# A four-layer image network on one Trainium2 core: in the last layer's recurrence, both channel halves share one tile of two PSUM banks, and the turn, copy and store of the results move one step on

## The chip, the cores and the metric

The program runs on one core of one Trainium2 chip. The metric is the device time of one execution in microseconds (us); lower is better. Shown are the median of three runs and one further execution that the hardware profiler recorded.

Engines: PE (TensorE, with its weight loads listed apart as PEld), DVE (VectorE), ACT (ScalarE), POOL (GpSimd) and SP (SyncE, which here only issues DMAs). Each takes its instructions in program order. [...]

## The reference

Four layers run one after the other on an image of shape 2 x 128 x 128 x 128 (fp32), each as `x + layer(group_norm(x))`. The change touches only the last one, a two-dimensional selective scan. Its centre, for each of 4 directions, 256 channels d and 16 states n:

```python
delta = softplus(dts + bias)
def step(h, (ut, dt, bt, ct)):
    h = exp(dt * A) * h + (dt * ut) * bt
    y = einsum('bkdn,bkn->bkd', h, ct)
```

The four directions are two orders of the pixels (rows first, columns first), each forward and backward. The four results are brought back to pixel order and added.

## The kernel before

`program` (L1768) calls the layers in turn. The recurrence is `layer3_scan` (L1228 to L1650). It works through 256 **parts** of 512 pixels: 2 images, 2 orders, forward and then backward, 16 strips, 2 halves of a strip. So the parts come in eight runs of 32: forward (`k` 0 or 1) and backward (`k` 2 or 3) by turns. This document calls the forward parts *plain* and the backward ones *turned*, because only the backward ones are turned to pixel order at their end: a plain part's result goes to scratch `yc` in DRAM as it is, and a backward part reads it again (`yf`), adds it, turns the sum with PE transposes (`unturn`), copies it out of PSUM on ACT and stores it to `ys` (`store`).

A part is 8 **slots**. A slot scans 4 tiles of 128 rows (32 channels x 4 states) x 512 pixels. Slot number `s` within a part is 2*q + e: q picks four of the 16 states, e the half of the 256 channels. One turn of the loop over `g` (L1632) issues, in this order:

1. the steps placed at "head";
2. `exponentials(g+1)`: four ACT Exp operations (L1544), tile `da`, from `db`;
3. `kept(g-1)`: an ACT copy of the last column of the finished scans to `states` (L1620), which waits for DVE's scans of slot g-1;
4. the steps at "mid";
5. `products(g+2)`: `but` = delta*u times b, mostly on ACT (L1568, six or seven a slot), the rest on POOL (L1563, one or two a slot). Slots 2q and 2q+1 both read the tiles made for both, so slot 2q needs what is issued only one turn earlier;
6. `weighted(g-1)`: POOL multiplies `hs` by c (L1626);
7. `tiles(g)`: for each j of 4, PE turns four pieces of `but` into one PSUM bank `ups` (L1600, three banks), DVE scans it (L1608), then the steps placed at j follow;
8. `sums(g-2)`: PE adds up the states into `yps` (L1582);
9. the steps at "end".

`in_order` (L114) fixes this order on every engine. The other work is a table of steps `(r, place, step)`: step of part i is issued in turn g = 8i + r. Since a part is 8 turns, r modulo 8 tells the slot of the scan beside which it runs; "slot 5" below means that slot of whichever part is being scanned. In order:

- `load_x` (-15), `load_u` (-10): DMAs in. `project(0)`, `project(1)` (-10, places 1 and 2): PE matmuls to `xdps` (L1332); `projected` (-9, head): ACT copy to `xd` (L1341) and the DMA of `cd`.
- `turn_b`, `ranks(0)`, `ranks(1)` (-8): PE to `btps` (L1350) and `dtps` (L1364). `softplus_a` (-7, head): on ACT two Abs (L1375), one Exp (L1376). `turned_b` (L1357), `softplus_b` (L1382): DVE. `softplus_c` (-6, mid): ACT Ln (L1388).
- `softplus_d(0)`, `(1)` (L1396), `softplus_e(0)`, `(1)` (L1403) in slot 2 and `softplus_f(0)`, `(1)` (L1412) in slot 3: DVE, one operation for each channel half, in place on `dtps` and then on `dl`. `spread` (-5, place 2): DMAs `dl` to DRAM `dd` and back, spread over the partitions, to `db` (L1424); likewise `cd` to `cb`.
- `turn(0)`, `turn(1)` (-4): PE transposes of `dl` to `dltps` (L1439). `turned(0)`, `turned(1)` (-3, slot 5): DVE, `du` = u times `dltps` (L1449).
- `load_forth` (6, end): `yf`. `skip(0)`, `skip(1)` (9 and 10, place 3): DVE, to `ysb` (L1471 plain, L1476 turned).
- `unturn(0)`, `unturn(1)` (13, places 2 and 3: slot 5): for plain parts the `yc` DMA, for turned parts eight PE transposes to `ytps` (L1500). `store` (14, head: slot 6), turned parts only: two ACT copies to `yt` (L1510) and the `ys` DMA (L1513).

PSUM: `ups` has 3 banks, `yps` 2, and pool `ps_m` 3 banks under one tag "misc", taken in turn by `xdps`, `btps`, the two `dtps`, the two `dltps` and the two `ytps`. A tile that comes fourth waits until the readers of the first are done.

Of the kernel before, what the change touches and what calls it, by code (L numbers as in the profile page):

```python
# [9 lines left out]
F32 = mybir.dt.float32  # L10
AF = mybir.ActivationFunctionType
ALU = mybir.AluOpType
PSUM = bass.MemoryType.PSUM
DRAM = bass.MemoryType.DRAM

P = 128
# [96 lines left out]
@contextmanager  # L113
def in_order(tc):  # L114

    cur = tc.nc.cur_bb
    first = len(cur.bb.instructions)
    mark = cur.bb.instructions[first - 1]
    yield
    assert tc.nc.cur_bb is cur  # L120
    traced = list(cur.bb.instructions)
    start = next(k for k in reversed(range(len(traced))) if traced[k] is mark) + 1
    last = {}
    for i in traced[start:]:
        prev = last.get(i.engine)
        if prev is not None:
            tc.add_manual_dep(
                i, prev.name,
                mybir.DependencyInfo(mybir.DependencyClass.NoSync, mybir.DependencyReason.DATA),
                reason="in_order",  # L130
            )
        last[i.engine] = i
# [1095 lines left out]
def layer3_scan(tc, cs, ins, xs, xst, yc, ys):  # L1228
# [11 lines left out]
    nc = tc.nc  # L1240
    NS, DR, NX, T = 16, 8, 40, 512
    with ExitStack() as ctx:
        pool = lambda name, bufs, **kw: ctx.enter_context(tc.tile_pool(name=name, bufs=bufs, **kw))
        w = pool("l3b_w", 1)
        one = pool("l3b_one", 1)
        two = pool("l3b_two", 2)
# [2 lines left out]
        five = pool("l3b_five", 5)  # L1249
        ps_u = pool("l3b_ps_u", 3, space=PSUM)  # L1250
        ps_y = pool("l3b_ps_y", 1, space=PSUM)
        ps_m = pool("l3b_ps_m", 3, space=PSUM)
        dr = pool("l3b_dr", 3, space=DRAM)
        tc.keep_in_program_order(
            nc.scalar.preload_act_table_set("natural_log_exp_and_others")
# [7 lines left out]
        dtw = w.tile([65, 4, 256], F32, name="dtw")  # L1263
        nc.sync.dma_start(dtw, ins["dt_ext"])
        xds = []
        for i in range(2):
            t = w.tile([65, T], F32, name=f"xd{i}")
# [25 lines left out]
        held = {}  # L1293

        def tag_of(i):
            return "_".join(map(str, parts[i]))
# [57 lines left out]
        def turned_b(i):  # L1354
            v = held[i]
            v["bt"] = two.tile([P, 4, NX], F32, name=f"bt_{tag_of(i)}", tag="bt")
            nc.vector.tensor_copy(v["bt"], v["bps"])  # L1357

        def ranks(e):
            def f(i):  # L1360
                k = parts[i][1]
                v = held[i]
                ps = ps_m.tile([P, T], F32, name=f"dtps_{tag_of(i)}_{e}", tag="misc")
                nc.tensor.matmul(  # L1364
                    ps, dtw[:, k, e * P : (e + 1) * P], v["xd"], start=True, stop=True
                )
                v.setdefault("dps", []).append(ps)
            return f


        def softplus_a(i):
            v = held[i]
            ae = one.tile([P, 2, T], F32, name=f"ae_{tag_of(i)}", tag="ae")
            for e in range(2):
                nc.scalar.activation(ae[:, e, :], v["dps"][e], AF.Abs)  # L1375
            nc.scalar.activation(ae, ae, AF.Exp, scale=-1.0)  # L1376
            v["ae"] = ae

# [9 lines left out]
            nc.scalar.activation(dl, v["up"], AF.Ln)  # L1388
            v["dl"] = dl

        def softplus_d(e):

            def f(i):
                v = held[i]
                ps = v["dps"][e]
                nc.vector.scalar_tensor_tensor(ps, ps, 0.0, v["ae"][:, e, :], ALU.max, ALU.add)  # L1396
            return f

        def softplus_e(e):
            def f(i):  # L1400
                v = held[i]
                ps = v["dps"][e]
                nc.vector.scalar_tensor_tensor(  # L1403
                    ps, v["up"][:, e, :], -1.0, ps, ALU.add, ALU.subtract
                )
            return f

        def softplus_f(e):
            def f(i):
                v = held[i]  # L1410
                dl = v["dl"][:, e, :]
                nc.vector.tensor_tensor(dl, dl, v["dps"][e], ALU.subtract)  # L1412
            return f

        def spread(i):

# [15 lines left out]
        def turn(g):  # L1432
            def f(i):
                v = held[i]
                tps = ps_m.tile([P, 2, 2, P], F32, name=f"dltps_{tag_of(i)}_{g}", tag="misc")
                for j in range(2):
                    for e in range(2):
                        p0 = (2 * g + j) * P
                        nc.tensor.transpose(tps[:, j, e, :], v["dl"][:, e, p0 : p0 + P], cs.ident)  # L1439
                v.setdefault("tps", []).append(tps)  # L1440
            return f

        def turned(g):

            def f(i):
                v = held[i]
                if g == 0:
                    v["du"] = two.tile([P, 4, 256], F32, name=f"du_{tag_of(i)}", tag="du")
                nc.vector.tensor_tensor(  # L1449
                    v["du"][:, 2 * g : 2 * g + 2, :], v["ut"][:, 2 * g : 2 * g + 2, :],  # L1450
                    v["tps"][g].rearrange("p j e d -> p j (e d)"), ALU.mult,
                )
            return f

        def load_forth(i):

# [6 lines left out]
        def skip(e):  # L1463
            def f(i):
                k = parts[i][1]
                v = held[i]
                if e == 0:
                    v["ysb"] = one.tile([P, 2, T], F32, name=f"ysb_{tag_of(i)}", tag="ysb")
                ysb, yps = v["ysb"], v["yps"]
                if k < 2:  # L1470
                    nc.vector.scalar_tensor_tensor(  # L1471
                        ysb[:, e, :], v["xc"][:, e, :], dsk[:, 0, k, e : e + 1], yps[e],
                        ALU.mult, ALU.add,
                    )
                else:
                    nc.vector.tensor_tensor(ysb[:, e, :], v["yf"][:, e, :], yps[e], ALU.add)  # L1476
            return f

        def pixels_of(i):


            b, k, s, sub = parts[i]
            i0 = 8 * s + 4 * sub
            if k % 2 == 0:
                return ys[b, 0].rearrange("(i j) d -> j i d", j=P)[:, i0 : i0 + 4, :]
            return ys[b, 1].rearrange("(j i) d -> j i d", i=P)[:, i0 : i0 + 4, :]

        def unturn(g):
            def f(i):
                b, k, s, sub = parts[i]  # L1490
                if k < 2:
                    if g == 0:
                        nc.sync.dma_start(yc[b, k, s, sub], held.pop(i)["ysb"])
                    return
                v = held[i]
                tps = ps_m.tile([P, 2, 2, P], F32, name=f"ytps_{tag_of(i)}_{g}", tag="misc")
                for j in range(2):
                    for e in range(2):
                        p0 = (2 * g + j) * P
                        nc.tensor.transpose(tps[:, j, e, :], v["ysb"][:, e, p0 : p0 + P], cs.ident)  # L1500
                v.setdefault("ytps", []).append(tps)
            return f

        def store(i):
            if parts[i][1] < 2:
                return
            v = held.pop(i)
            yt = one.tile([P, 4, 256], F32, name=f"yt_{tag_of(i)}", tag="yt")
            for g in range(2):
                nc.scalar.copy(  # L1510
                    yt[:, 2 * g : 2 * g + 2, :], v["ytps"][g].rearrange("p j e d -> p j (e d)")
                )
            nc.sync.dma_start(pixels_of(i), yt)  # L1513


# [3 lines left out]
            (-10, 1, project(0)), (-10, 2, project(1)), (-9, "head", projected),  # L1519
            (-8, 0, turn_b), (-8, 1, ranks(0)), (-8, 2, ranks(1)),  # L1520
            (-7, "head", softplus_a), (-7, 0, turned_b), (-7, 2, softplus_b),
            (-6, "mid", softplus_c), (-6, 0, softplus_d(0)), (-6, 1, softplus_d(1)),
            (-6, 2, softplus_e(0)), (-6, 3, softplus_e(1)),
            (-5, 0, softplus_f(0)), (-5, 1, softplus_f(1)), (-5, 2, spread),
            (-4, 0, turn(0)), (-4, 1, turn(1)), (-3, 0, turned(0)), (-3, 1, turned(1)),
            (6, "end", load_forth), (9, 3, skip(0)), (10, 3, skip(1)),
            (13, 2, unturn(0)), (13, 3, unturn(1)),
            (14, "head", store),
        ]

        def at(g, place):
# [97 lines left out]

        slots = 8 * len(parts)  # L1630
        with in_order(tc):
            for g in range(-15, slots + 7):  # L1632
                at(g, "head")
                if 0 <= g + 1 < slots:
                    exponentials(g + 1)
                if 0 <= g - 1 < slots:
                    kept(g - 1)
                at(g, "mid")
                if 0 <= g + 2 < slots:
                    products(g + 2)  # L1640
                if 0 <= g - 1 < slots:
                    weighted(g - 1)
                if 0 <= g < slots:
                    tiles(g)
                else:
                    for j in range(4):
                        at(g, j)
                if 0 <= g - 2 < slots:
                    sums(g - 2)
                at(g, "end")  # L1650
# [230 lines left out]
```

## Time and profile before

| | us |
|---|---|
| median of 3 runs (18427.80 to 18434.36) | 18432.44 |
| profiled execution | 18430.42 |
| its span, first to last instruction | 18428.6 |
| mean granted TensorE clock | 0.918 |

Busy time over the whole span: PE 14403.4 (78%), PEld 8312.0 (45%), DVE 15967.4 (87%), ACT 14862.3 (81%), POOL 11820.0 (64%).

The recurrence lies between about 6200 and 17920 us of the span; the 40 slices of the page show DVE, ACT and POOL at 9 tenths through all of it. Within one run of 32 parts the profile is periodic, with about 45 us a part, and the eight runs differ only by their kind.

How to read the lines further down. A group's line gives the code line, engine, operation, output <- input, shapes and count; after the first bar busy time and the mean ns of one; after the second the engine's idle time just before them and what ended it. A timeline's line gives the start (us), how long it took, the engine, the code line and operation, how many alike follow one another, and in brackets the idle time before and what ended it. Operations on one engine overlap a little at their ends, so the distance from start to start is shorter than the recorded length. A window's line gives, for a stretch of time, each engine's busy time and instruction count, the clock that was granted to TensorE (1.00 is full) and the DMA load.

### The profile page before, as it was taken

What the parts mean: (1) busy time and instruction counts of PE and PEld (TensorE: products, weight loads), DVE (VectorE), ACT (ScalarE), POOL (GpSimd) and SP (SyncE); (2) the same over time, 40 slices, a digit from 0 to 9 for tenths busy, and PEclk for the clock granted to TensorE, in tenths of its full rate; (3) what the DMA queues carried; (4) which work ended last, traced back from release to release, by engine and by line L of the source; (5) the groups of instructions that cost most, each with busy time, mean ns of one, the idle gap of its engine ahead of it and who ended that gap; (6) DMA issues with size and microseconds to landing.
All of it is one profiled execution on the core that took longest, in us unless ns stands there. A gap on an engine that the chain in (4) does not pass through costs nothing. (4 is left out here: it accounts for less than half of the span.)

```text
span 18428.6 us, 277686 instructions
## 1 busy us (share of the span) xinstructions
PE 14403.4 (78%) x97794; PEld 8312.0 (45%) x97794; DVE 15967.4 (87%) x20729; ACT 14862.3 (81%) x30049; POOL 11820.0 (64%) x6490
## 2 busy tenths in 40 slices
PE   7888888887568777777777777777777777777778
PEld 5555555664223344444444444444444444344445
DVE  5776666336889899999999999999999999999996
ACT  4665666334455799999999999999999999999984
POOL 0000000011000499999999999999999999999981
PEclk9999999889779889999999999999999999999989
DMA  2000000111114544444444455544444444445546
GB/s 44 24 23 23 16 18 15 61 64 56 56 48 163 164 116 117 123 126 129 126 115 115 115 126 128 129 123 120 115 122 127 127 124 119 121 118 129 127 129 192
DMA packets 1232639, 1859.34 MB, mean 101 GB/s; under 512 B 124877, under 2 KB 591565, under 8 KB 1228942
## 3 DMA queue, kind: packets, MB, share of 16 engines
q1 hardware_dynamic: 1157374, 1817.40, 37.3%
q10 hardware_dynamic: 73872, 24.16, 0.5%
q8 instruction: 777, 12.73, 0.3%
q14 instruction: 616, 5.05, 0.1%
HBM read 1396.64 MB, written 444.60 MB: 100 GB/s over the span
## 5 line engine op out<-in xcount | busy, mean ns | idle before, releaser
L1608 DVE TENSOR_TENSOR_SCAN hs<-da,states,ups 128x512 f32<-128x512 f32 x8192 | 9926.5, 1266 | 259.9 <-PE ups L1600 248.6
L1626 POOL TENSOR_TENSOR hs<-hs,cb 128x2048 f32<-128x2048 f32 x2048 | 9407.3, 4593 | 314.1 <-POOL but L1563 184.1
L1600 PE MATMUL ups<-ident,but 128*128 128x128 f32 x32768 | 5573.6, 301 | 2587.5 <-DVE hs L1608 1726.5
L1600 PEld LDWEIGHTS ups<-ident,but 128*128 128x128 f32 x32768 | 3865.2, 150 | 6191.5 <-DVE hs L1608 3549.3
L1568 ACT ACTIVATE but<-du,bt 128x256 f32<-128x256 f32 x12800 | 5329.2, 498 | 5.1 <-DVE du L1449 4.2
L1544 ACT ACTIVATE da<-db,na 128x512 f32<-128x512 f32 x8192 | 5224.8, 710 | 24.1 <-DMA db<-dd 20.0
L1582 PE MATMUL yps<-hs,sel 128*32 128x512 f32 x16384 | 2484.5, 682 | 61.4 <-POOL hs L1626 47.6
L1563 POOL TENSOR_TENSOR but<-du,bt 128x256 f32<-128x256 f32 x3584 | 2150.1, 621 | 17.7 <-DVE du L1449 17.7
L306 POOL TENSOR_TENSOR xres<-xres,rowb 128x256 f32<-128x256 f32 x128 | 94.5, 739 | 2445.8 <-DMA xres<-in_x 1810.3
L391 ACT COPY pT<-tps 128x512 f32<-128x512 f32 x1280 | 722.1, 584 | 1115.8 <-PE tps L386 1115.8
L386 PE MATMUL tps<-ident,s 128*128 128x128 f32 x8192 | 1228.9, 287 | 433.5 <-DVE pT L389 269.3
L358 DVE CUSTOM_DVE_ANT_1 s<-sps,relbias 128x512 f32<-128x512 f32 x2048 | 1321.6, 683 | 138.9 <-PE sps L341 133.6
L386 PEld LDWEIGHTS tps<-ident,s 128*128 128x128 f32 x8192 | 900.2, 144 | 1028.7 <-issue 499.6
L371 ACT ACTIVATE s<-s,nm 128x1024 f32<-128x1024 f32 x1024 | 1163.7, 1138 | 129.7 <-DVE nm L369 126.6
L1139 POOL MEMSET xpad<- 128x34 f32 x8 | 1.3, 162 | 1242.7 <-PE xs L1030 1178.8
L341 PE MATMUL sps<-kc,qT 32*128 32x512 f32 x4096 | 619.8, 673 | 1.9 <-DVE qT L326 1.2
L1620 ACT COPY states<-hs 128x4 f32<-128x4 f32 x2048 | 381.5, 186 | 273.3 <-DVE hs L1608 273.3
L389 DVE COPY pT<-tps 128x512 f32<-128x512 f32 x768 | 528.2, 688 | 57.3 <-PE tps L386 54.9
L1582 PEld LDWEIGHTS yps<-hs,sel 128*32 128x32 f32 x16384 | 339.5, 114 | 485.7 <-issue 303.4
L1332 PE MATMUL xdps<-xc,xpw 128*40 128x512 f32 x1024 | 540.5, 610 | 12.4 <-POOL xd L1269 12.4
L1364 PE MATMUL dtps<-xd,dtw 65*128 65x512 f32 x1024 | 539.8, 609 | 0.0
L734 POOL TENSOR_TENSOR xr<-xr,row_ln_b 128x512 f32<-128x512 f32 x64 | 81.1, 1269 | 705.4 <-DMA xr<-x 312.5
(287 smaller groups left out, 16213.1 us busy)
## 6 DMA issues: line engine op xcount, KB each, us to landing
db<-dd SPq DMA_DIRECT2D x1024, 512.0 KB
cb<-cd SPq DMA_DIRECT2D x1024, 256.0 KB
xc<-xs SPq DMA_DIRECT2D x256, 512.0 KB
dd<-dl SPq DMA_DIRECT2D x256, 512.0 KB
ut<-xst SPq DMA_DIRECT2D x128, 512.0 KB
yc<-ysb SPq DMA_DIRECT2D x128, 512.0 KB
yf<-yc SPq DMA_DIRECT2D x128, 512.0 KB
ys<-yt SPq DMA_DIRECT2D x128, 512.0 KB
```

The lines of the kernel that those rows point to most:

```text
L341: nc.tensor.matmul(sps, v["qT"][hp, qt * P : (qt + 1) * P], kc[b, wh + g][hp, ww : ww + 2].rearrange("p a r c -> p (a r c)"), start=True, ...
L358: nc.vector.tensor_tensor_reduce(blocks(v["s", qt][:, h, 512 * g : 512 * g + 512]), blocks(v["sps", qt, g][h]), bias[:, h, :, r0 : r0 + WS ...
L371: nc.scalar.activation(s[:, h, :], s[:, h, :], AF.Exp, bias=nm[:, 2, h : h + 1], scale=-1.0, accum_out=v["sums"][:, qt, h : h + 1],)
L386: nc.tensor.transpose(tps[:, j, :], v["s", qt][:, h, k0 : k0 + P], cs.ident)
L391: nc.scalar.copy(dst, tps)
L1544: nc.scalar.activation(da[:, j, :], held[i]["db"][:, 4 * e + j, :], AF.Exp, scale=na[:, k, c : c + 1])
L1563: nc.gpsimd.tensor_tensor(but[:, j, :, n, :], du[:, tb], bt[:, tb, c : c + 1].unsqueeze(2).to_broadcast([P, 8, 32]), ALU.mult,)
L1568: nc.scalar.activation(but[:, j, :, n, :], du[:, tb], AF.Copy, scale=bt[:, tb, c : c + 1])
L1582: nc.tensor.matmul(v["yps"][e][32 * j : 32 * j + 32, :], sel, hs[:, j, :], start=(q == 0), stop=(q == 3),)
L1600: nc.tensor.transpose(ups[:, tb * P : (tb + 1) * P], v[("but", q, tb // 2)][:, tb % 2, 4 * e + j].rearrange("p n c -> p (n c)"), cs.ident,)
L1608: nc.vector.tensor_tensor_scan(o, a, u, state[:, c0 + j : c0 + j + 1], ALU.mult, ALU.add)
L1626: nc.gpsimd.tensor_tensor(hs, hs, v["cb"][:, s // 2, :].unsqueeze(1).to_broadcast([P, 4, T]), ALU.mult)
```

## The change

`ps_m` keeps one bank "misc" for `xdps` and `btps`; its other two banks become one tile "pair" (`two_banks`), held by `dtps`, then `dltps`, then `ytps`. Each of these now has both halves in one tile, and every pair of operations that read them becomes one operation over 1024 columns: one Abs on ACT, one each of softplus_d, e and f and of `turned` on DVE, one `yt` copy on ACT. The matmuls and transposes stay what they were in number and size.

Steps that merge take the first one's place: d at (-6, 0), e at (-6, 2), f at (-5, 0), turned at (-3, 0). `unturn(0)`, `unturn(1)` go from (13, 2) and (13, 3) to (14, 0) and (14, 1), that is from slot 5 to slot 6, where `project(0)` (place 1, listed earlier, so ahead of `unturn(1)`) and `project(1)` (place 2) run too. `store` goes from the head of slot 6 to the head of slot 7, behind `projected`. The loop runs one turn longer.

```diff
-        ps_m = pool("l3b_ps_m", 3, space=PSUM)
+        ps_m = pool("l3b_ps_m", 1, space=PSUM)
...
+        def two_banks(i, name):
+            return ps_m.tile([P, 2, T], F32, name=f"{name}_{tag_of(i)}", tag="pair")
...
-                ps = ps_m.tile([P, T], F32, name=f"dtps_{tag_of(i)}_{e}", tag="misc")
+                if e == 0:
+                    v["dps"] = two_banks(i, "dtps")
                 nc.tensor.matmul(
-                    ps, dtw[:, k, e * P : (e + 1) * P], v["xd"], start=True, stop=True
-                )
-                v.setdefault("dps", []).append(ps)
+                    v["dps"][:, e], dtw[:, k, e * P : (e + 1) * P], v["xd"], start=True, stop=True
+                )
...
-            for e in range(2):
-                nc.scalar.activation(ae[:, e, :], v["dps"][e], AF.Abs)
+            nc.scalar.activation(ae, v["dps"], AF.Abs)
...
+            nc.vector.scalar_tensor_tensor(ps, ps, 0.0, v["ae"], ALU.max, ALU.add)
...
+            nc.vector.scalar_tensor_tensor(ps, v["up"], -1.0, ps, ALU.add, ALU.subtract)
...
+            nc.vector.tensor_tensor(v["dl"], v["dl"], v["dps"], ALU.subtract)
...
+            nc.vector.tensor_tensor(flat(v["du"]), flat(v["ut"]), flat(v["tps"]), ALU.mult)
...
-            for g in range(2):
-                nc.scalar.copy(
-                    yt[:, 2 * g : 2 * g + 2, :], v["ytps"][g].rearrange("p j e d -> p j (e d)")
-                )
+            nc.scalar.copy(flat(yt), flat(v["ytps"]))
             nc.sync.dma_start(pixels_of(i), yt)
...
-            (-6, "mid", softplus_c), (-6, 0, softplus_d(0)), (-6, 1, softplus_d(1)),
-            (-6, 2, softplus_e(0)), (-6, 3, softplus_e(1)),
-            (-5, 0, softplus_f(0)), (-5, 1, softplus_f(1)), (-5, 2, spread),
-            (-4, 0, turn(0)), (-4, 1, turn(1)), (-3, 0, turned(0)), (-3, 1, turned(1)),
+            (-6, "mid", softplus_c), (-6, 0, softplus_d), (-6, 2, softplus_e),
+            (-5, 0, softplus_f), (-5, 2, spread),
+            (-4, 0, turn(0)), (-4, 1, turn(1)), (-3, 0, turned),
             (6, "end", load_forth), (9, 3, skip(0)), (10, 3, skip(1)),
-            (13, 2, unturn(0)), (13, 3, unturn(1)),
-            (14, "head", store),
+            (14, 0, unturn(0)), (14, 1, unturn(1)),
+            (15, "head", store),
...
-            for g in range(-15, slots + 7):
+            for g in range(-15, slots + 8):
```

## The prediction

> **What bounds the kernel now.** I read the page's busy times, then its groups, then windows over the eight runs of the recurrence (32 parts each), then ACT's, DVE's and PE's own timelines. The groups name the load of one slot: four scans, one big product on POOL, about six ACT products beside four exponentials.
>
> ```profile
> L1608 DVE TENSOR_TENSOR_SCAN hs<-da,states,ups 128x512 f32<-128x512 f32 x8192 | 9926.5, 1266 | 259.9 <-PE ups L1600 248.6
> L1626 POOL TENSOR_TENSOR hs<-hs,cb 128x2048 f32<-128x2048 f32 x2048 | 9407.3, 4593 | 314.1 <-POOL but L1563 184.1
> L1568 ACT ACTIVATE but<-du,bt 128x256 f32<-128x256 f32 x12800 | 5329.2, 498 | 5.1 <-DVE du L1449 4.2
> ```
>
> ```profile
> 6250.00:7707.00 1457.00, 1122.85 (x6775) 602.23 (x6774) 1429.47 (x1406) 1405.85 (x3033) 1417.01 (x702) 0.91 0.46 116
> 7707.00:9164.00 1457.00, 1136.33 (x6994) 616.84 (x6995) 1423.91 (x1401) 1428.65 (x3088) 1417.75 (x701) 0.93 0.49 128
> ```
>
> The window columns are PE, PEld, DVE, ACT, POOL, granted clock, DMA share, GB/s. The first window holds plain parts (k<2), the second turned parts (k>=2, with L1500 and L1510). DVE, ACT and POOL are all 96 to 98% busy, so none alone is the bound. The end is set by a loop that changes engine: ACT waits for DVE at the state copy (L1620), DVE waits for PE's `ups`, and PE waits for ACT's `but`. One turned part, ACT, then DVE:
>
> ```profile
> 8546.74 0.20 ACT L1620 COPY states<-hs 128x4 f32<-128x4 f32 x1 [0.64 <-DVE hs L1608]
> ...
> 8554.19 1.04 ACT L1510 COPY yt<-ytps 128x512 f32<-128x512 f32 x2
> 8555.14 2.56 ACT L1544 ACTIVATE da<-db,na 128x512 f32<-128x512 f32 x4
> 8557.60 0.19 ACT L1620 COPY states<-hs 128x4 f32<-128x4 f32 x1
> ...
> 8560.10 0.57 ACT L1341 COPY xd<-xdps 40x512 f32<-40x512 f32 x1
> 8560.56 2.57 ACT L1544 ACTIVATE da<-db,na 128x512 f32<-128x512 f32 x4
> ...
> 8592.14 0.20 ACT L1620 COPY states<-hs 128x4 f32<-128x4 f32 x1 [0.49 <-DVE hs L1608]
> ```
>
> ```profile
> 8554.83 16.53 DVE L1608 TENSOR_TENSOR_SCAN hs<-da,states,ups 128x512 f32<-128x512 f32 x14
> 8571.68 1.28 DVE L1608 TENSOR_TENSOR_SCAN hs<-da,states,ups 128x512 f32<-128x512 f32 x1 [0.33 <-PE ups L1600]
> ...
> 8578.44 1.28 DVE L1608 TENSOR_TENSOR_SCAN hs<-da,states,ups 128x512 f32<-128x512 f32 x1 [0.55 <-PE ups L1600]
> ```
>
> ACT has no wait from the state copy in slot 4 (8546.74) until its products let DVE start slot 2 at 8578.44; from there DVE has none until the next such copy. Both stretches are on the path. A plain part closes the loop at the copy in slot 6 instead. Median distance of two starts of slot 2, over 112 parts of each kind: 45.31 us plain, 45.52 turned.
>
> **The merged operations.** On DVE a pair of 512-wide operations on `dtps` or `dltps` costs 2 x 0.58 (start to next start). The nearest 1024-wide one out of two banks is L978, 1193 ns against 674 for L1396, so 0.52 more: 1.10 for the pair, 0.05 to 0.06 saved. Four pairs (d, e, f, turned), all in DVE's stretch: 0.22 a part. Bounds: nothing saved, or 0.1 each. On ACT the Abs pair takes 1.10; one 1024-wide copy out of PSUM takes 1003 ns (L1032), so 1.04 with the gap to Exp: 0.06 saved in ACT's stretch. The yt pair goes from 0.95 to 0.90. Plain parts have nothing else on the path: -0.28 each, 128 of them, **-36 us** (bounds -10 and -60).
>
> [...]
>
> **The deltas' hand-over.** f ends after one scan of slot 3 instead of two, so `dd` leaves SP about 1.3 us earlier. In 14 parts ACT waited at slot 7 for the late `db`; with what followed they cost 48 us over the usual part. Nearly all waited under 1.3 beyond usual, so I take **-48** (bounds 0 and -48).
>
> **The buffers.** `pair` passes from dtps (freed by f, slot 3) to dltps (slot 4; it needs f anyway) to ytps (slot 6; turned ends in slot 5) to the next ranks in slot 0, some 5 us after the yt copy of slot 7. `xdps` and `btps` in the one `misc` bank are half a part apart. All waits are covered: 0, else 1 us for each us of a missing cover, since PE's ups stand behind. On SP the ys store passes load_u and load_forth (slot 6) and stands behind the cd store; its readers are in the next layer. The yc store goes half a slot later, with 19 us until ysb is rewritten. The added last slot is under 1 us.
>
> **The moved turn and copy** touch turned parts only. Take the part above.
> 1. Without the yt pair in slot 6, ACT reaches the copy of slot 6 at 8557.60 - 0.95 = 8556.65. The scan it needs ends at 8554.83 + 1.17 + 1.27 - 0.05 = 8557.22. So ACT waits; of the 0.95 only 0.35 is kept.
> 2. PE now has four turns (0.59 by the steps of its rows) between project(0) and project(1). The second projection ended at 8559.36 (8558.31 + 1.05); it ends near 8559.36 + 0.59 - 0.05 = 8559.90, and ACT, ready for xd at 8559.75, waits 0.2. xd starts at 8559.95 instead of 8560.10.
> 3. The single yt copy follows: the exponentials start at 8561.31 instead of 8560.56, **+0.75**, and ACT has no idle time to give it back before slot 2. DVE starts slot 2 at 78.44 + 0.75 - 0.06 = 8579.13.
> 4. Loop: 8557.22 to 8579.13 is 21.91; DVE went from 8578.44 to the end of slot 5 (8600.35 + 1.17 + 1.27 = 8602.79) in 24.35, now 24.35 - 0.22 = 24.13. Together 46.04, +0.52 on 45.52; times 128 **+66 us** (bounds +0.35 and +0.6 a part: without and with PE's delay).
>
> So far 18430.4 - 36 - 48 + 66 = 18412. The profiled execution took 18430.42 (span 18428.6), 2 us below the median, so the sum stands for the runs as well.
>
> **What is late next: PE's clock.** The 0.75 lengthens PE's wait for the last `but` ahead of slot 0. Ordinary part, then one in which `db` came late:
>
> ```profile
> 8564.77 0.55 PE L1600 MATMUL ups<-ident,but 128*128 128x128 f32 x3
> 8566.08 0.33 PE L1600 MATMUL ups<-ident,but 128*128 128x128 f32 x1 [0.76 <-ACT but L1568]
> ```
>
> ```profile
> 7923.83 0.33 PE L1600 MATMUL ups<-ident,but 128*128 128x128 f32 x1 [1.20 <-ACT but L1568]
> ```
>
> ```profile
> 7921.21:7924.62 3.41, 2.21 (x17) 0.96 (x10) 2.98 (x4) 3.41 (x9) 3.41 (x1) 1.00 1.08 335
> 7924.62:7928.04 3.42, 3.42 (x11) 2.27 (x11) 2.21 (x2) 3.42 (x9) 3.42 (x4) 0.50 0.87 329
> ```
>
> ```profile
> 7933.63 1.28 DVE L1608 TENSOR_TENSOR_SCAN hs<-da,states,ups 128x512 f32<-128x512 f32 x1 [1.66 <-PE ups L1600]
> ...
> 7937.40 1.82 DVE L1382 TENSOR_SCALAR up<-ae 128x1024 f32<-128x1024 f32 x1
> ```
>
> After the 1.20 us wait the granted clock is 0.50: slot 0 runs at half speed, DVE stalls for `ups`, and softplus_b (670 ns otherwise) then starts behind a POOL product and takes 1.82. The clock records change on a fixed grid of 3.41 us. Over all parts, twelve wait 1.2 us here; eight of them get 0.50 in slot 0. None of those that wait less does (usually 0.76 in turned, 0.47 in plain parts; three between 1.11 and 1.18). The four turned parts among the eight lasted 50.0 to 51.3 us: less 45.5 and their own lateness, 4.6 us for a halved clock.
>
> After the change: the three transposes end 0.23 later (slot 7's first scan waits for PE), the fourth starts 0.75 later: 0.76 + 0.75 - 0.23 = 1.28 us of wait, in every turned part. Whether it tips depends on where the grid falls. 1.28 is at the edge of the group, so I take two fifths, below the eight in twelve: 0.4 x 128 x 4.6 = **+236**. Bounds: a fifth (+118), two thirds (+395). Sum: 18412 + 236 = 18648, said as **18650**.
>
> [...] The rows show the halving after 1.20 us, so I follow them.
>
> **Rivals.** (1) PE stays warm: the turns moved to slot 6 fill its window. For it: the three waits of 1.11 to 1.18 kept the full clock, and without PE's 0.2 in step 2 the wait is 1.08. It decides if the wait stays under 1.2. Then 18412, no change that counts; chance 0.20. (2) Faster: the copy falls into a hole, because ACT is not held at slot 6 and its stretch is not longer. It decides if the copy of slot 6 still follows its scan by 0.3 us; then both kinds gain 0.28 and the 48: 18430 - 72 - 48 = 18310. Against it: the state copy of slot 6 in plain parts, without yt, does wait. Chance 0.08. (3) Nearly every turned part runs slot 0 at half clock: 18412 + 589 = 19000; chance 0.10.
>
> **The numbers.** The forecast has 0.62. Its own range is 18530 to 18810. To hold 8 in 10 the range takes in rival 1 and the forecast's upper bound with the other terms' bounds: 18400 to 18860; rivals 2 and 3 stay out. About 0.2% (37 us) is what a measurement of this kernel can tell from no change. Slower by more: 0.62 and 0.10, 0.72. Within: most of rival 1, 0.16. Faster: rival 2 and rival 1's lower edge, 0.12.
>
> **What would show it.** DVE: dtps and du operations 128x1024 near 1.2 us, plain parts at 45.0. ACT: a wait for hs at slot 6 of turned parts, xd and then yt in slot 7. PE: the last `ups` of slot 0 waiting about 1.2 us; granted clock 0.50 in slot 0 of many turned parts, with long L1382. If turned parts last 46.0 without halved clocks, rival 1 holds; if they last 45.2, step 1 was wrong.

## The result, and the profile after

The changed kernel took **18510.43 us** (median of five runs, 18504.32 to 18513.97); the kernel before took 18427.80 (five runs, 18401.62 to 18434.36). The ratio is **1.0048, 95% interval 1.0036 to 1.0059**: slower, as forecast, but by 83 us and not by the 218 of the sum. The profiled execution has a span of 18508.6 us, 80 over that of before, at a mean granted clock of 0.902 (before 0.918).

The group of the scan, from the page, answers to the first line shown of before: DVE's idle time ahead of the scans rose from 259.9 to 333.1 us, and PE ended nearly all of it.

```profile
L1599 DVE TENSOR_TENSOR_SCAN hs<-da,states,ups 128x512 f32<-128x512 f32 x8192 | 9879.2, 1263 | 333.1 <-PE ups L1591 306.1
```

The windows over the first (plain) and second (turned) run of the recurrence, as shown of before (PE, PEld, DVE, ACT, POOL, granted clock, DMA share, GB/s):

```profile
6250.00:7707.00 1457.00, 1134.50 (x6833) 611.24 (x6836) 1438.35 (x1295) 1422.97 (x3042) 1436.55 (x710) 0.90 0.46 116
7707.00:9164.00 1457.00, 1139.10 (x6854) 623.77 (x6847) 1399.34 (x1246) 1400.18 (x2958) 1389.24 (x686) 0.89 0.49 125
```

In the plain run POOL's busy time went from 1417.01 to 1436.55 us in the same 1457: more parts passed. In the turned run it went from 1417.75 to 1389.24 at a clock of 0.89 instead of 0.93: fewer passed. So plain parts gained and turned parts lost.

The end of one turned part on ACT: the state copy of slot 6, the products, `xd`, the single `yt` copy, the exponentials of slot 7, and the products ahead of slot 0.

```profile
7948.86 0.20 ACT L1611 COPY states<-hs 128x4 f32<-128x4 f32 x1 [0.68 <-DVE hs L1599]
...
7951.39 0.58 ACT L1341 COPY xd<-xdps 40x512 f32<-40x512 f32 x1
7951.87 1.01 ACT L1504 COPY yt<-ytps 128x1024 f32<-128x1024 f32 x1
7952.78 2.56 ACT L1535 ACTIVATE da<-db,na 128x512 f32<-128x512 f32 x4
...
7955.33 2.90 ACT L1559 ACTIVATE but<-du,bt 128x256 f32<-128x256 f32 x7
```

The same part on PE: the second pair of turns, what follows it, and slot 0.

```profile
7949.28 0.65 PE L1492 MATMUL ytps<-ident,ysb 128*128 128x128 f32 x4
7949.77 0.60 PE L1591 MATMUL ups<-ident,but 128*128 128x128 f32 x4
7950.30 1.05 PE L1332 MATMUL xdps<-xc,xpw 128*40 128x512 f32 x2
...
7956.58 0.55 PE L1591 MATMUL ups<-ident,but 128*128 128x128 f32 x3
7958.29 0.33 PE L1591 MATMUL ups<-ident,but 128*128 128x128 f32 x1 [1.16 <-ACT but L1559]
...
7958.92 0.66 PE L1591 MATMUL ups<-ident,but 128*128 128x128 f32 x4
...
7960.72 1.06 PE L1591 MATMUL ups<-ident,but 128*128 128x128 f32 x4
7961.57 1.92 PE L1368 MATMUL dtps<-xd,dtw 65*128 65x512 f32 x2
```

PE waits 1.16 us for the last `but` ahead of slot 0. The first four transposes behind the wait still take 0.66 us, the next four 1.06. The windows on the grid of 3.41 us show the granted clock:

```profile
7956.39:7959.81 3.42, 2.26 (x17) 1.46 (x14) 3.16 (x3) 3.42 (x8) 3.42 (x1) 1.00 0.81 299
7959.81:7963.22 3.41, 3.41 (x8) 1.65 (x7) 2.64 (x3) 3.37 (x9) 3.41 (x4) 0.50 0.00 2
```

In the first stretch PE was busy for 2.26 of 3.42 us, and the wait lies in it; in the second the clock is 0.50. DVE then stalls, and softplus_b (L1384) takes 2.48 us:

```profile
7967.15 1.28 DVE L1599 TENSOR_TENSOR_SCAN hs<-da,states,ups 128x512 f32<-128x512 f32 x1 [1.42 <-PE ups L1591]
...
7970.92 2.48 DVE L1384 TENSOR_SCALAR up<-ae 128x1024 f32<-128x1024 f32 x1
```

Over all parts (period from start of slot 2 to the next, counted to the part it ends in, in us; "long" is over 48 us, "usual" is the mean of the others):

| | plain: usual, long | turned: usual, long | sum plain | sum turned |
|---|---|---|---|---|
| before | 45.32, 4 of 127 | 45.47, 6 of 128 | 5778.6 | 5848.8 |
| changed | 45.01, 0 | 45.73, 28 of 128 at 50.31 | 5715.9 | 5982.2 |

In all 28 the granted clock is 0.50 in slot 0, and in none of the other 100. Plain parts: -63 us. Turned parts: +133. Together +70 of the span's +80. Another 9 lie ahead of the first scan, which starts at 6241.1 instead of 6232.5; over all ten profiles told of here besides that of before, where the code ahead of it does not differ in anything that should matter, it starts between 6223.1 and 6241.4, so I take this for scatter.

The late `db` is gone. ACT's waits for `db`, before and after, in us, times, longest:

```profile
ACT da L1544 <- DMA db<-dd: 20.0, 15, 10.0
```

```profile
ACT da L1535 <- DMA db<-dd: 8.3, 1, 8.3
```

One wait in each is that of the very first part (10.0 and 8.3); the other fourteen of before are missing after.

### The profile page after: what moved, and what is told of

It is laid out like the page before. It is cut to its first block, busy times and chain, and to the rows that moved or that the text cites. A ratio compares the mean times of both kernels' runs of the same rounds, so it can differ in the third digit from the quotient of the medians.

```text
span 18508.6 us, 276280 instructions
## 1 busy us (share of the span) xinstructions
PE 14532.6 (79%) x97794; PEld 8424.0 (46%) x97794; DVE 15963.7 (86%) x19705; ACT 14865.3 (80%) x29665; POOL 11834.5 (64%) x6490
## 5 line engine op out<-in xcount | busy, mean ns | idle before, releaser
L1599 DVE TENSOR_TENSOR_SCAN hs<-da,states,ups 128x512 f32<-128x512 f32 x8192 | 9879.2, 1263 | 333.1 <-PE ups L1591 306.1
L1591 PEld LDWEIGHTS ups<-ident,but 128*128 128x128 f32 x32768 | 3948.0, 152 | 6056.6 <-DVE hs L1599 3505.7
L1573 PE MATMUL yps<-hs,sel 128*32 128x512 f32 x16384 | 2566.8, 703 | 65.0 <-POOL hs L1617 65.0
```

The source lines that it names most:

```text
L1573: nc.tensor.matmul(v["yps"][e][32 * j : 32 * j + 32, :], sel, hs[:, j, :], start=(q == 0), stop=(q == 3),)
L1591: nc.tensor.transpose(ups[:, tb * P : (tb + 1) * P], v[("but", q, tb // 2)][:, tb % 2, 4 * e + j].rearrange("p n c -> p (n c)"), cs.ident,)
L1599: nc.vector.tensor_tensor_scan(o, a, u, state[:, c0 + j : c0 + j + 1], ALU.mult, ALU.add)
```

## The experiments

My theory after seeing the result: the signs of all the prediction's terms are right, and the loss is the half clock in slot 0, brought on by PE's wait ahead of it, which the `yt` copy lengthens. The rivals were that the place of the turn alone decides, that the half clock has another cause than this wait (the rhythm of the parts on the grid), and that the late `db` went by the later store. Each ratio below is to the kernel before, timed on the same chip.

### The old place with the merged tile

```diff
-            (14, 0, unturn(0)), (14, 1, unturn(1)),
-            (15, "head", store),
+            (13, 2, unturn(0)), (13, 3, unturn(1)),
+            (14, "head", store),
```

> All merged operations and the shared pair of banks stay; the turn, copy and store go back to where they were (turn in slot 5, copy and store at the head of slot 6). Theory (the move costs, by the longer wait of PE and the halved clock; the merging gains): plain parts 45.0 us as in the changed kernel, turned parts 45.2 instead of 45.5 before (0.28 saved, half of it perhaps not), no granted clock of 0.50 in slot 0, no late db. Ratio to the kernel before 0.992 to 0.995. Rival (the merged tile is what costs, because turns and deltas now wait for one another in two banks): 1.003 or more, with waits of PE or ACT on dltps, ytps or dtps.

Measured: 18729.50 us, ratio 1.0165 (1.0149 to 1.0180). The expectation was wrong in sign, and its rival held. Usual turned parts took 46.54 us, and 61 of 128 were long, each with a granted clock of 0.50 in slot 0, in most behind a wait of PE of 1.21 us. The timeline of PE in slot 5 and that of ACT in slot 6, then ACT's waits for the turn in the recurrence:

```profile
7809.48 0.67 PE L1492 MATMUL ytps<-ident,ysb 128*128 128x128 f32 x4 [1.63 <-DVE du L1444]
...
7810.80 1.06 PE L1492 MATMUL ytps<-ident,ysb 128*128 128x128 f32 x4
```

```profile
7811.90 1.01 ACT L1504 COPY yt<-ytps 128x1024 f32<-128x1024 f32 x1 [1.92 <-PE ytps L1492]
```

```profile
ACT yt L1504 <- PE ytps L1492: 165.8, 120, 2.3
```

The results' tile needs the pair that `turned` still reads, so PE stands 1.63 us for DVE with the next `ups` queued behind it, the second four turns take 1.06 us instead of 0.67 (granted clock 0.50 from 7809.99 to 7813.40), and the one copy has to wait for both halves: 120 times, 165.8 us. So the step further on cannot simply be left out of the change: the shared pair needs it, or at least a later place than the old one.

### The new place with single operations

```diff
-            (13, 2, unturn(0)), (13, 3, unturn(1)),
-            (14, "head", store),
+            (14, 0, unturn(0)), (14, 1, unturn(1)),
+            (15, "head", store),
```

> The kernel before, with only the turn, copy and store moved one step on; all operations stay single. Theory: turned parts without a halved clock go from 45.5 to about 46.1 (the copy in slot 7 takes 0.95 and nothing is saved elsewhere), a quarter to a half of the turned parts have the clock halved in slot 0 and last 50 to 51, plain parts stay at 45.3, late db still occurs. Ratio 1.010 to 1.020. Rival (merged tile costs, the place does not): 0.998 to 1.003.

Measured: 18708.98 us, 1.0147 (1.0128 to 1.0167), as expected. Usual turned parts 46.08, 0.61 over those of before; 56 long ones at 50.30. PE's wait ahead of slot 0 is 1.20 us in most. The fourteen waits for `db` are still there (10.4 us), and plain parts stay at 45.33, twelve of them long. Against the changed kernel this shows what the merged operations, with the earlier deltas that come of them, are worth when the place is the same: a ratio of 1.0147 against 1.0048.

### The copy behind the products

```diff
-            (15, "head", store),
+            (15, "end", store),
```

> The changed kernel, with the copy and the store at the end of slot 7 instead of its head, so ACT makes the products that PE waits for ahead of the copy. ACT's stretch from slot 6 to slot 2 stays as long. Theory (a quarter of the turned parts is long only because PE's wait ahead of slot 0 grows to 1.16 us and its clock is halved): that wait falls back to 0.4 to 0.7 us, no halved clock in slot 0, turned parts all 45.7 to 45.9, plain 45.0, ratio 0.995 to 0.998. Rival (ACT's lateness alone makes the long parts, wherever the copy stands ahead of slot 2): long parts stay, ratio 1.003 to 1.006.

Measured: 18389.44 us, 0.9974 (0.9965 to 0.9983), as expected. The copy now follows the last product ahead of slot 0, so PE waits 0.26 us there instead of 1.16:

```profile
7944.60 2.91 ACT L1559 ACTIVATE but<-du,bt 128x256 f32<-128x256 f32 x7
7947.40 1.00 ACT L1504 COPY yt<-ytps 128x1024 f32<-128x1024 f32 x1
```

```profile
7947.55 0.33 PE L1591 MATMUL ups<-ident,but 128*128 128x128 f32 x1 [0.26 <-ACT but L1559]
```

No part is long. Usual turned parts take 45.83: the copy still has its length on ACT. Why they take 0.10 more than in the changed kernel, the runs do not tell. So the 28 long parts do not come from the copy's length but from where it makes PE wait.

### Work for PE in the wait

The copy stays where the change put it; in the first tile of slot 0, behind turned results only, PE does six transposes more: those of the first two quarters, three times over, into the place in `ups` where they were written already.

```diff
-                for tb in range(4):
+                again = s == 0 and j == 0 and i >= 2 and parts[i - 2][1] >= 2
+                for tb in ((0, 1, 2, 0, 1, 0, 1, 0, 1, 3) if again else range(4)):
```

> The changed kernel, with six transposes more on PE in its wait ahead of slot 0, after turned results only: they write the same two quarters of ups again with the same numbers (about 0.9 us of PE's time, inside the wait of 1.16 us). ACT and DVE keep their work. Theory (the clock is halved because PE does too little in one stretch of its 3.41 us grid): no granted clock of 0.50 in slot 0, no part over 48 us, turned parts 45.7 to 45.8, ratio 0.995 to 0.998. Rival (the clock is not the cause, or is set by something other than PE's own work): long parts stay, ratio 1.004 or more.

Measured: 18386.94 us, 0.9973 (0.9962 to 0.9983), as expected. PE does more work, and the ratio falls from 1.0048 to 0.9973:

```profile
7954.23 1.20 PE L1592 MATMUL ups<-ident,but 128*128 128x128 f32 x9
7955.95 0.33 PE L1592 MATMUL ups<-ident,but 128*128 128x128 f32 x1 [0.51 <-ACT but L1559]
```

Usual turned parts 45.78, no long one. The last `but` comes no earlier here (6.36 us from the start of the `yt` copy to its end in both kernels, median), and only PE's idle time is shorter. This shows the cause: the 128 turned parts went from 5982.2 to 5859.5 us when 0.65 us of PE's idle time ahead of slot 0 was filled.

### Less of the fill, and a longer wait

One transpose more instead of six, then no fill but a small operation behind the copy:

```diff
+                for tb in ((0, 1, 2, 0, 3) if again else range(4)):
```

```diff
             nc.scalar.copy(flat(yt), flat(v["ytps"]))
+            nc.scalar.copy(idle, idle)
```

> The changed kernel with one transpose more in PE's wait ahead of slot 0 of turned parts (the third quarter's product is turned a second time into the same place of ups, in each of the four tiles' first one only), so that the wait becomes about 1.0 us instead of 1.16. Theory (the halved clock depends on how long PE is without work ahead of slot 0, and 1.16 us lies just over the point): 0 to 14 of 128 turned parts over 48 us instead of 28; ratio to the kernel before 0.997 to 1.001. Rival (the halving has another cause than this wait, for instance the fixed rhythm of the parts against the grid of 3.41 us): 20 to 40 parts stay long, ratio 1.003 to 1.006.

> The changed kernel with one small ACT copy (128x4, about 0.19 us) of an otherwise unused tile behind the copy of yt, so that the exponentials, and with them the last product ahead of slot 0, come 0.15 to 0.2 us later in turned parts: PE's wait becomes about 1.3 us, which is what the prediction expected of the change. Theory (the size of the wait sets the share of halved parts): 40 to 75 of 128 turned parts over 48 us, the others at about 45.9; ratio 1.007 to 1.016. Rival (the locked rhythm of one in four is set by the grid and not by the size of the wait): 24 to 36 long ones, ratio 1.005 to 1.0065 by the 0.15 us a part alone.

The transpose that is repeated is that of the first quarter, not of the third as the expectation says, and only in the first tile of the slot. Measured: 18422.24 us, 0.9990 (0.9981 to 0.9999), and 18586.18 us, 1.0078 (1.0064 to 1.0092). PE's waits ahead of slot 0, first with one transpose more, then with the later exponentials:

```profile
7955.00 0.33 PE L1592 MATMUL ups<-ident,but 128*128 128x128 f32 x1 [1.05 <-ACT but L1559]
```

```profile
7945.54 0.33 PE L1594 MATMUL ups<-ident,but 128*128 128x128 f32 x1 [1.21 <-ACT but L1562]
```

At 1.05 us 5 of 128 turned parts are long, at 1.16 (the changed kernel) 28, at 1.20 41; the usual part stays within 45.73 to 45.81 in the three. The small operation lengthened the wait by 0.04 us only, where 0.15 was expected, so that the count still came into the expected range (41 of 40 to 75) is partly luck. The rivals' counts (20 to 40, and 24 to 36) held in neither. That a few tip at 1.05, that most do not at 1.20, and that 56 did in the kernel with single operations at the same 1.20, shows that the wait alone does not decide a part.

The traces show what else does: where the wait falls on the clock's grid. I lay the grid of 3.413 us through the times at which the recorded clock changes, and take how far behind an edge the first transpose after the wait begins (in the lines above 7958.29, 1.90 us behind 7956.39). In the changed kernel this is 1.73 to 1.92 us in all 28 halved parts; of the other 96 parts with a wait over 1 us, none has a value between 0.99 and 2.07. PE's busy time in the stretch does not tell them apart: 34 of those 96 have the same 2.25 or 2.26 us. At a wait of 1.05 us the halved parts lie between 1.73 and 1.80, at 1.20 between 1.09 and about 2.2, so a longer wait widens the range that tips.

### Softplus_f in two halves again

```diff
-            (-5, 0, softplus_f), (-5, 2, spread),
+            (-5, 0, softplus_f(0)), (-5, 1, softplus_f(1)), (-5, 2, spread),
```

> The changed kernel with softplus_f again as two operations, one behind each of the first two scans of slot 3, so that the deltas leave a scan later. Theory of the prediction (the late db of the kernel before came from this, 48 us): 10 to 14 waits of ACT for db come back, with 4 or more plain parts over 48 us; ratio to the kernel before 1.005 to 1.009, that is 0.001 to 0.003 over the changed kernel. Rival (the late db went because the store of the results now lies half a slot later on SP and in the queues): no such wait, no long plain part, ratio as for the changed kernel, 1.004 to 1.0055.

Measured: 18553.05 us, 1.0059 (1.0046 to 1.0072). The interval overlaps that of the changed kernel, so the time alone does not tell the two theories apart; the waits do. ACT's waits for `db`, the first part's 8.6 us among them:

```profile
ACT da L1538 <- DMA db<-dd: 18.1, 14, 8.6
```

Thirteen late `db` are back; their parts lie 40 us over their kind's usual time. Eight plain parts are long, five of them at a late `db`. The usual plain part is 45.10 instead of 45.01, one pair's saving among it. The recurrence, first to last scan, takes 11793.0 us instead of 11746.5. These 46 us are not the late `db` alone: the lost saving of one pair lies in them too, and four long turned parts fewer (24 instead of 28). The store lies as late as in the changed kernel, so the rival falls.

### The copy in the hole

Both turns go behind the last scan of slot 5, when `turned` has left the pair; the copy goes on ACT between the exponentials and the state copy of slot 6, where the changed kernel waits 0.68 us for DVE.

```diff
-            (14, 0, unturn(0)), (14, 1, unturn(1)),
-            (15, "head", store),
+            (13, 3, unturn(0)), (13, 3, unturn(1)),
+            (14, "gap", store),
...
                     exponentials(g + 1)
+                at(g, "gap")
```

> The changed kernel, but with both turns behind the last scan of slot 5 (PE), and the single copy of yt on ACT behind the exponentials of slot 6 and ahead of the state copy of slot 6, where ACT of the changed kernel waits 0.68 us for DVE. Theory (in the changed kernel the copy costs its length because it lies between xd and the exponentials, in a stretch of ACT that has no idle time, and it lengthens PE's wait ahead of slot 0 to 1.16 us): here most of its 0.9 us falls into the wait of slot 6, so turned parts come to about 45.2 to 45.4 us, PE's wait ahead of slot 0 to about 0.7, no turned part keeps half a clock in slot 0; ratio 0.993 to 0.997. Rival (any place one step earlier is too early for the shared pair, as where the turn stood at its old place: PE waits for DVE's product 'turned', and the copy for PE): the copy waits over 1 us, the exponentials of slot 7 are later by as much, ratio 1.003 or more.

Measured: **18322.59 us, 0.9934 (0.9921 to 0.9946)**, as expected: faster than both kernels.

```profile
7883.56 2.55 ACT L1535 ACTIVATE da<-db,na 128x512 f32<-128x512 f32 x4
7886.02 0.99 ACT L1504 COPY yt<-ytps 128x1024 f32<-128x1024 f32 x1
7886.91 0.20 ACT L1611 COPY states<-hs 128x4 f32<-128x4 f32 x1
7887.01 2.51 ACT L1559 ACTIVATE but<-du,bt 128x256 f32<-128x256 f32 x6
7889.42 0.56 ACT L1341 COPY xd<-xdps 40x512 f32<-40x512 f32 x1
7889.88 2.56 ACT L1535 ACTIVATE da<-db,na 128x512 f32<-128x512 f32 x4
```

The state copy follows the `yt` copy with no wait, so most of the copy fell into the old wait, and the exponentials follow `xd` at once. Usual turned parts take 45.28 and plain ones 44.99; in the ordinary turned part PE waits 0.76 us ahead of slot 0, as before the change. Two turned parts are long (50.1 us), neither with a half clock in slot 0: in both, softplus_b began 0.2 us behind the start of a POOL product and took 4.86 and 4.92 us instead of 0.67.

The same place with the single operations of the kernel before, for the share of the place:

```diff
-            (13, 2, unturn(0)), (13, 3, unturn(1)),
-            (14, "head", store),
+            (13, 3, unturn(0)), (13, 3, unturn(1)),
+            (14, "gap", store),
```

> The kernel before with its single operations and its three banks in turn, but with both turns behind the last scan of slot 5 and the two yt copies on ACT behind the exponentials of slot 6, ahead of the state copy, as in e5_gap_copy. Theory (the gain of e5_gap_copy comes from the merged operations: in the kernel before the copies of slot 6 already lay in ACT's wait for DVE, so their place gives nothing): turned parts stay at 45.4 to 45.6 us, plain parts at 45.3, the late db stay; ratio 0.998 to 1.002. Rival (the gain comes from the place, behind the exponentials): turned parts come to 45.2 to 45.3 us without any merging; ratio 0.994 to 0.997.

Measured: 18436.02 us, 0.9997 (0.9988 to 1.0006), as expected: usual turned parts 45.48, plain ones 45.36, eighteen late `db`.

```profile
7957.69 2.55 ACT L1544 ACTIVATE da<-db,na 128x512 f32<-128x512 f32 x4
7960.14 1.04 ACT L1510 COPY yt<-ytps 128x512 f32<-128x512 f32 x2
7961.08 0.20 ACT L1620 COPY states<-hs 128x4 f32<-128x4 f32 x1
```

Here too the state copy follows without a wait, as it did in the kernel before. The place gives nothing by itself; the gain of 0.66% is that of the merged operations and the earlier deltas, in a place that does not spoil it.

## Why the prediction was right and wrong

The forecast named the right chain and the right sign, and was wrong in size: one term was nearly twice too large, and another just twice. The measured time also lies just below the forecast's own range (18530 to 18810), in the part that had been added for rival 1. Its terms beside what the two profiles show, in us; the measured ones split the parts' times into usual and long, so they add up by construction:

| term of the sum | forecast | measured | how measured |
|---|---|---|---|
| merged operations, plain parts | -36 | -39 | usual plain part 45.32 to 45.01, x 127 |
| late `db` | -48 | -44 | the eight long parts of before in which ACT waited ahead of slot 7's exponentials, over their kind's usual one: 4 x 5.8 + 4 x 5.2 |
| two other long parts of before | none | -8 | 49.4 each, full clock in slot 0, softplus_b 4.97 us |
| moved turn and copy, clock full | +66 | +33 | usual turned part 45.47 to 45.73, x 128 |
| half clock in slot 0 | +236 | +128 | 28 x 4.58 |
| recurrence | +218 | +70 | |

**The step that failed** is the last: "1.28 is at the edge of the group, so I take two fifths", the term of +236 that measured +128. The price of one halved part was right (4.58 against 4.6), and so was the chain behind it: a half clock in slot 0, DVE's stall for `ups`, a long softplus_b. The count was not: 28 of 128, 22%, not 51. Three things are in it. The wait was 1.16 us, not 1.28, and the two kernels with 1.05 and 1.20 show how steeply the count falls there (5 and 41). The forecast left it open where the grid falls and took a share as if by chance; in the changed kernel only parts whose wait ends 1.73 to 1.92 us behind an edge of the grid tip, and for most of a run that is every fourth. And the share of eight in twelve that I came down from was taken from parts in which a late `db` had delayed other work as well; no run separates what that added. The 22% lies just above the forecast's lower bound of a fifth.

The row with the halving after 1.20 us was the one to follow: behind waits of 1.16 us the changed kernel has 28 halved parts, and filling 0.65 us of that wait took away all 28.

**The second size, the moved turn and copy.** Step 1 held: ACT waits 0.68 us at the state copy of slot 6. Step 3 held: `yt` follows `xd` and takes 0.91 from start to start. Step 2 failed: PE's four turns were to delay `xd` by 0.2 us, and ACT waits for nothing there, in this part (`xd` starts at 7951.39, right behind the products) as in all others. The four turns take 0.49 (7949.28 to 7949.77), not 0.59, and the second projection ends at 7951.35, just ahead of `xd`. Then step 4 took DVE's stretch from the one part shown, 24.35, where the median of the usual turned parts was 24.24. Measured medians: 21.79 from the end of slot 5 to the next slot 2, and 23.98 from there back, together 45.77 against the forecast's 46.04. The lower bound "without PE's delay" (+0.35) was still a little above the measured +0.26. This missing 0.2 also more than covers why the wait was 1.16 and not 1.28; the prediction named 1.08 for that case.

**The merged operations** were sized right: 0.31 a plain part against 0.28. In the turned part before the one shown, a merged operation takes 1.12 on DVE from start to start, where two single ones took 1.16:

```profile
7925.86 1.21 DVE L1397 SCALAR_TENSOR_TENSOR dtps<-dtps,ae 128x1024 f32<-128x1024 f32 x1
7926.98 2.44 DVE L1599 TENSOR_TENSOR_SCAN hs<-da,states,ups 128x512 f32<-128x512 f32 x2
```

**The late `db`** was right, in size (-44 against -48) and in cause: the split softplus_f brought thirteen of them back.

**Rival 1** (PE keeps the full clock, 18412) was to decide if the wait stayed under 1.2. It did, at 1.16, and yet 28 parts were halved: the reading that no part with a shorter wait tips rested on three waits of 1.11 to 1.18 that kept the full clock, too few to set the bound. The rival describes what the other four fifths of the turned parts do: the changed kernel with PE's wait filled is 18386.94, ratio 0.9973. Rival 2's condition, the copy in a hole, did not hold in the changed kernel, since ACT is held at slot 6 as step 1 said. Where it was made to hold, the kernel took 18322.59, close to the 18310 worked out for it.

## What to carry to other kernels

Where one engine stands between two others, one operation over a shared larger tile can take less time than two over its halves (here 1.12 us against 1.16 on DVE, 0.31 us in a plain part of 45.32), but the tile ties its users together (with the turn at its old place ACT waited 120 times for it, 165.8 us): look first for who still holds it, then for the wait into which the later step can fall. Before costing a moved copy at its length, find the idle time on its engine and put it there: with the turn and the single copy at one place the kernel was 0.5% slower than before, at another 0.7% faster. A wait of 1.16 us on PE was not free here even though PE had time to spare (busy for 79% of the span): behind it 28 of 128 parts had a clock of 0.50 and took 4.58 us more. Look at the granted clock in the stretch behind such a wait; if it drops, some idle work in the wait can be a cure (here 1.0048 came down to 0.9973).

## What the runs showed of the hardware

**The half clock came behind waits of about 1 us.** Ahead of slot 0, waits of 1.05, 1.16 and 1.20 us of PE brought 5, 28 and 41 of 128 parts to a granted clock of 0.50; at 0.26, 0.51 and the 0.76 of the ordinary part in the kernel with the copy in the hole, none. In the part shown the wait ends in a stretch in which PE was busy for about two thirds (2.26 of 3.42 us); as the experiments show, it is the place of the wait on the grid that tells such a part from the others (its end 1.73 to 1.92 us behind an edge in all 28 of the changed kernel).

**The halved parts come in a rhythm.** In the changed kernel every fourth turned part is long for most of a run (parts 38, 42, 46, 50, 54, 58, 62). From part 38 to part 62 four parts take 187.5 to 187.9 us, 187.7 on the mean, and 55 steps of the clock's grid (3.413 us) are 187.7, so each fourth part meets the grid at nearly the same point, inside the range that tips. That the long part itself holds the rhythm by this match is argued, not shown.

**A delayed DVE operation can fall behind a POOL product.** In the halved part POOL's product ran as softplus_b began:

```profile
7968.31 4.54 POOL L1617 TENSOR_TENSOR hs<-hs,cb 128x2048 f32<-128x2048 f32 x1 [1.40 <-issue]
```

It ended at 7972.85, and softplus_b, begun at 7970.92, ended 0.55 later; alone it takes 0.67. In the part before, softplus_b began first (7921.72), and POOL's product, from 7921.90, took 4.89, where the products ahead of it and behind it took 4.56. Why each takes longer beside the other, no run shows. Of the 4.58 us of a halved part, 3.25 are lost up to the first scan of slot 1 (8.91 us after the last `but` instead of 5.66); softplus_b, 1.8 us longer than usual, more than covers the rest.

Nine parts show the delay beside a POOL product alone: two of the kernel before, two with the copy in the hole, two in the same place with single operations and three with softplus_f in two halves. Their clock is full in slot 0, and softplus_b, begun 0.1 to 0.2 us behind the start of a POOL product of 4.5 us, takes 4.86 to 4.97 us; the parts last 49.1 to 50.1. In every other part of the eleven profiles softplus_b takes 0.67 us, or the clock was halved in slot 0.
